# A graph layer on one core: products in four runs a block, float32 work in three, and fewer edges by gather

## The chip, the cores and the metric

The kernel runs on one core of a Trainium2 chip. The metric is the device time of one execution in microseconds; times are compared as medians of several runs on the same chip. TensorE appears in the profile as PE (its matmuls) and PEld (its loads of the stationary operand), VectorE as DVE, ScalarE as ACT, GpSimd as POOL, and the queue that issues most transfers as SP.

## The reference

A graph with 6250 nodes of 64 features and 206250 edges, sorted by their target node `dst`. Each edge carries the normalised features of its source node and 64 features of its own; both are summed into the target node, and a small network follows.

```python
h = jnp.maximum(_layernorm(x, axis=-1), 0.0)
msg = h[src] + edge_attr_64
agg = jax.ops.segment_sum(msg, dst, num_segments=6250)
out = x + jax.nn.relu(agg @ W1 + b1) @ W2 + b2
```

All values are float32; `W1` is 64 x 128, `W2` 128 x 64.

## The kernel before, in words

The sum over edges is split by node. For the first 5502 nodes the source features are not fetched at all. Instead the kernel counts, for three target nodes at a time (a *tile*, a window of up to 128 edges), how many edges come from each of the 6250 nodes, and multiplies these counts by the feature table. For the last nodes the 25 last groups of 1024 edges are gathered from the table by GpSimd (8 gathers a group, each added onto the edge's own features) and summed by matmuls.

The main loop runs over 308 steps of 6 tiles, 14 steps to a *block* of 252 nodes, 22 blocks. A step is written n, its place in the block s (0 to 13). All engines take their instructions in an order that this loop writes out by hand (`tc.manual_schedule`), so the order of the calls in the code is the order in each engine's queue. In a step:

- `count(n)` (L805): six fp8 matmuls of one-hot rows give the counts in `pc`, which has two buffers of PSUM; ACT copies them into `ring` (L811, "eviction" below). The one-hot rows are made by DVE, 18 tiles at a time, every third step (`rows_of_tiles`, L791; every sixth step `encode` comes ahead of it, L772 and L778).
- `products(b - 1, ...)` (L823): 49 matmuls a block in float32r multiply the counts of the block before by the table `h2` into `pv`. `PART` says which of them go into which of the steps 1 to 8. At step 9 DVE adds `pv` to the sums (`add_products`, L852). The ring is long enough that steps 0 to 8 of the next block write to free places.
- The edges' own features: `chunk_hot` (L392, DVE) and `chunk_sum` (L405, 48 float32 matmuls for two chunks of 42 nodes) at s = 6 and 7, 9 and 10, 12 and 13 gather a block's sums in `bank`. `take_sums` (L412, ACT) copies them out at the next block's step 0, and `chunk_place` (L428) adds them to `pv` at its step 2.
- `turn` (L647, L648 on PE; L654, L658 on ACT) brings the codes of 128 tiles into `kq` and `kv`; it stands at steps with s in `TURNS` = (0, 7): in blocks 1 to 21 eight at 0 and five at 7. The codes are unpacked by DVE in the four steps before (`unpack`).
- The small network (`mlp`): `mlp_hidden` (L893, ACT L895), `mlp_product` (L901), `mlp_add` (L906, DVE) and `mlp_store` (L910, SP), one block of nodes at a time, begun at s = 2 or 9 with the later parts 2, 3 and 4 steps on. `residual(g)` loads x for four blocks into one of two slots and `add_b2` adds the bias; the sum goes into one of two buffers `ys`.
- `features_h` (DVE L447, PE L451, ACT L454; the sums are added later at L439) sums two gathered groups, at s = 5 or 11 once the plan says that they have landed. It then queues the gathers of the next two groups on GpSimd (`fetch_h`, L266); the edges' features for them are loaded on SP (`load_h`, L916). The planned clock counts `STEP_US` a step and `GATHER_US` a gather.

After the loop come the products of the last block, cut into fours with the placing and the rest between, then the last group, `add_products`, and the network for the last two blocks of nodes.

Of the kernel before, what the change touches and what calls it, by code (L numbers as in the profile page):

```python
# [22 lines left out]
P = 128  # L23
# [29 lines left out]
GP = 25  # L53
GA = G - GP
EA = GA * P * J

# [17 lines left out]
TURNS = (0, 7)  # L74
TILES = NW * BT
# [29 lines left out]
STEP_US = 1.4  # L105
# [8 lines left out]
def gnn_kernel(ctx: ExitStack, tc: tile.TileContext, x, src_t, dst_t, dst_g, edge, w1, b1, w2, b2, out):  # L114
    nc = tc.nc

    start = [b * BN - (NX * V if b > SB else 0) for b in range(NW)] + [NS]
# [4 lines left out]
    assert max(pairs) == NP and 2 * sum(pairs) == N and start[NW] == NS  # L122
# [245 lines left out]
    for b in range(NW):  # L368
        c0, c1 = start[b] // CN, start[b + 1] // CN
        units += [(b, c, min(c1 - c, GB), i) for i, c in enumerate(range(c0, c1, GB))]  # L370
# [43 lines left out]
    def at_columns(b, a, z):  # L414

        if b % 2 == 0:
            return [(a, z, a)]
        cut = FRESH * SC
        runs = [(a, min(z, cut), a + BN - cut), (max(a, cut), z, max(a, cut) - cut)]
        return [run for run in runs if run[0] < run[1]]  # L420

    def chunk_place(u):
        b, c, n, i = units[u]
        for k in range(n):
            o = (c + k) * CN - start[b]
            at = (i * GB + k) * D
            for a, z, to in at_columns(b, o, o + CN):
                nc.tensor.matmul(pvs[b][k * D:(k + 1) * D, to:to + z - a], by_node[b][:, at:at + D],  # L428
                                 select[:, a - o:z - o], start=False, stop=False)

# [11 lines left out]
    def sum_groups(g, tiles):  # L442
        m = len(tiles)
        pa = bank[:, 512 - GB * W:].rearrange("p (b w) -> p b w", b=GB)
        for b in range(m):
            hot = spare["hotp"][b]
            nc.vector.tensor_tensor(hot, rel_p[:, g - GA + b, :].unsqueeze(2).to_broadcast([P, J, W]),  # L447
                                    iota[:, :W].unsqueeze(1).to_broadcast([P, J, W]), op=OP.is_equal)
            for j in range(J):
                k = j % 2 * D  # L450
                nc.tensor.matmul(pa[k:k + D, b, :], tiles[b][:, j, :], hot[:, j, :],  # L451
                                 start=(j < 2), stop=(j >= J - 2))
# [123 lines left out]
    nc.sync.dma_start(dst_p, dst_t.rearrange("p (g j) -> p g j", j=J)[:, GA:, :])  # L576

# [219 lines left out]
    def count(n):  # L797
# [9 lines left out]
        b, s = divmod(n, STEPS)  # L807
        c = (s if b % 2 == 0 else (STEPS if s < FRESH else 0) + s) * SC
# [8 lines left out]
    def products(b, a, z):  # L817

        if a == 0:
            pvs[b] = ps.tile([P, 512], F32, tag="pv", name="pv")[:, :BN]  # L820
        c = b % 2 * FRESH * SC
        for h in range(a, z):
            nc.tensor.matmul(pvs[b], h2[:, h, :], ring[:, h, c:c + BN], start=(h == 0), stop=(h == HI - 1))  # L823
# [16 lines left out]
    ys = [cut(2 * D)[:NP].rearrange("p (k d) -> p k d", k=2) for _ in range(2)]  # L840
    tail = cut(NX * V)
    spare["sum_p"] = cut(GB * W).rearrange("p (b w) -> p b w", b=GB)
    spare["by_node"] = cut(3 * GB * D)
    hids.append(spare["by_node"][:, :BN])
    spare["hotp"] = [cut(J * W).rearrange("p (j w) -> p j w", j=J) for _ in range(GB)]

    def add_products(b):
        pv = pvs.pop(b)
        n = start[b + 1] - start[b]
# [36 lines left out]
    turn_of = [0]  # L886

    def mlp_hidden(b, k=0):
        n = start[b + 1] - start[b]
        made[b >= NW] = start[b + 1]  # L890
        turn_of[0] ^= 1
# [359 lines left out]
```

## Time and profile before

| what | us |
|---|---|
| median of three runs | 495.16 (491.98 to 500.49) |
| profiled execution, its own time | 493.56 |
| its span, first to last instruction | 491.9 |
| PE busy | 413.5 (84%) |
| DVE busy | 351.4 (71%) |
| ACT busy | 349.7 (71%) |
| POOL busy | 386.9 (79%) |
| first count of the loop starts | 43.05 |
| last two counts of the loop start | 472.43 |

A line of the profile names engine, line of the code, operation, tiles written and read and their shapes; "x48" is the number of instructions merged into one row. In brackets stands how long the engine was idle ahead of it, and who ended that. In the timeline the first number is the start and the second the length; in the table of groups the numbers are busy time, mean length of one in ns, and idle time ahead with its releasers; in the table of waits they are total, times and the longest.

### The profile page before, as it was taken

How to read it: one execution, taken by the hardware profiler on the slowest of the kernel's cores; microseconds unless marked ns; L12 is line 12 of the kernel's file. 1: busy time of each engine (PE TensorE's matmuls, PEld its weight loads, DVE VectorE, ACT ScalarE, POOL GpSimd, SP SyncE). 2: the span in 40 equal slices, each digit the busy share in tenths (PEclk: the TensorE clock that was granted, in tenths of full speed). 3: DMA queues.
4: the chain of work that ended last, by engine and by line, in shares of the span. 5: the costliest groups of instructions: out<-in, count | busy, mean ns of one | idle time of the engine just before them, and what ended most of it. 6: DMA issues, size and time to landing. Idle time of an engine off the chain costs nothing.

```text
span 491.9 us, 17202 instructions
## 1 busy us (share of the span) xinstructions
PE 413.5 (84%) x7172; PEld 371.8 (76%) x7173; DVE 351.4 (71%) x772; ACT 349.7 (71%) x514; POOL 386.9 (79%) x272
## 2 busy tenths in 40 slices
PE   3014779988979997999999998999999989998984
PEld 3013668877878886987888897898888878887974
DVE  4799948985778756688577876698576776687531
ACT  3437977786756868777778798788687766786740
POOL 6756838888888588888888888888888888888880
PEclk9999889999899998999999999999999989999998
DMA  8929455676475848567577768568669567487610
GB/s 225 271 87 325 96 127 124 159 212 153 104 192 117 218 106 210 109 162 198 120 203 174 191 150 217 130 157 230 138 145 248 118 139 191 112 204 169 149 19 18
DMA packets 114099, 78.90 MB, mean 160 GB/s; under 512 B 33864, under 2 KB 109120, under 8 KB 113792
## 3 DMA queue, kind: packets, MB, share of 16 engines
q1 hardware_dynamic: 83624, 65.87, 44.6%
q0 software_dynamic: 30096, 10.36, 18.0%
q10 hardware_dynamic: 295, 1.52, 0.9%
q8 instruction: 58, 0.95, 0.8%
q14 instruction: 26, 0.20, 0.1%
HBM read 73.72 MB, written 3.99 MB: 158 GB/s over the span
## 4 chain that ended last, share of the span: by engine, by line
PE 60%; ACT 16%; DVE 14%; issue 5%; DMA 2%; POOL 1%; DVEq 0%; ACTq 0%
PE pv L823 24%; PE pc L805 19%; ACT ring L811 8%; PE bank L405 8%; DVE hot L791 3%; PE bank L451 3%; ACT kq L654 3%; PE ph L893 2%; PE pv L428 2%; DVE hotf L392 2%; ACT kv L658 2%; DMA sums<-in_dst_g,row_i 1%; DVE sums L852 1%; POOL sums L266 1%; PE po L901 1%
## 5 line engine op out<-in xcount | busy, mean ns | idle before, releaser
L266 POOL DMA_INDIRECT pfeat<-table,src_p x200 | 340.0, 1700 | 64.2 <-issue 53.9
L811 ACT ACTIVATE ring<-pc 128x882 fp32r<-128x882 f32 x308 | 275.1, 923 | 76.8 <-PE pc L805 73.5
L805 PE MATMUL pc<-hot 128*128 128x147 fp8e4 x1848 | 173.6, 234 | 25.4 <-ACT ring L811 13.7
L791 DVE TENSOR_TENSOR hot<-at,of 128x576 int32<-128x576 bf16 (+1 forms) x206 | 161.7, 826 | 29.9 <-PE pc L805 25.3
L823 PE MATMUL pv<-ring,h 128*128 128x252 f32 x1078 | 170.5, 295 | 1.5 <-ACT ring L811 1.5
L805 PEld LDWEIGHTS <-hot 128*128 128x128 fp8e4 x1848 | 127.6, 101 | 46.3 <-issue 20.7
L823 PEld LDWEIGHTS pv<-ring,h 128*128 128x128 f32 x1078 | 139.7, 192 | 1.8 <-ACT ring L811 1.7
L405 PE MATMUL bank<-feat,hotf 128*18 128x64 f32 x3144 | 59.5, 226 | 7.3 <-DVE hotf L392 5.6
L405 PEld LDWEIGHTS bank<-feat,hotf 128*18 128x18 f32 x3144 | 47.7, 101 | 16.4 <-DVE hotf L392 7.0
L852 DVE TENSOR_TENSOR sums<-sums,pv 128x252 f32<-128x252 f32 (+3 forms) x33 | 9.9, 327 | 58.2 <-PE pv L823 56.9
L392 DVE TENSOR_TENSOR hotf<-rel,iota 128x432 f32<-128x432 bf16 x66 | 39.5, 598 | 0.0
L654 ACT ACTIVATE kq<-pk 128x512 bf16<-128x512 f32 (+17 forms) x48 | 18.2, 442 | 17.3 <-PE pk L647 17.3
L772 DVE TENSOR_TENSOR at<-iota_a,kq 128x576 bf16<-128x576 bf16 (+1 forms) x52 | 23.3, 448 | 2.0 <-ACT kq L654 1.7
L778 DVE TENSOR_TENSOR of<-of,kv 128x432 bf16<-128x432 bf16 (+1 forms) x52 | 19.8, 381 | 3.0 <-ACT kv L658 0.2
L266 POOL DMA_INDIRECT words<-packed,first_i x15 | 18.2, 1213 | 4.6 <-issue 3.7
L893 PE MATMUL ph<-sums,w1s 128*128 128x252 f32 (+2 forms) x50 | 17.2, 430 | 5.0 <-ACT over L730 1.8
L266 POOL DMA_INDIRECT sums<-in_dst_g,row_i x15 | 15.4, 1030 | 6.7 <-issue 4.3
L772 DVE TENSOR_TENSOR of<-iota_w,kq 128x432 bf16<-128x432 bf16 (+1 forms) x52 | 19.3, 371 | 0.0
L906 DVE TENSOR_TENSOR after<-po,after 126x128 f32<-126x128 f32 (+2 forms) x25 | 7.2, 287 | 14.5 <-PE po L901 14.0
L454 ACT ACTIVATE after<-bank 128x84 f32<-128x84 f32 (+1 forms) x13 | 3.1, 239 | 19.9 <-PE bank L451 19.9
L895 ACT ACTIVATE after<-ph,b1s 128x252 f32<-128x252 f32 (+2 forms) x25 | 11.9, 475 | 5.3 <-PE ph L893 5.3
L451 PE MATMUL bank<-after,pfeat 128*64 128x42 f32 x400 | 14.5, 232 | 1.2 <-DVE after L447 1.2
(182 smaller groups left out, 315.0 us busy)
## 6 DMA issues: line engine op xcount, KB each, us to landing
feat<-in_edge SPq DMA_DIRECT2D x131, 384.0 KB
pfeat<-in_edge SPq DMA_DIRECT2D x25, 256.0 KB
pfeat<-table,src_p POOLq DMA_INDIRECT x200
out_y<-after SPq DMA_DIRECT2D x23, 63.0 KB
dstn<-in_dst_g SPq DMA_DIRECT2D x1, 1024.0 KB
table<-xl SPq DMA_DIRECT2D x2, 512.0 KB
after<-in_x SPq DMA_DIRECT2D x4, 252.0 KB
packed<-dstn ACTq DMA_DIRECT2D x1, 768.0 KB
```

The lines of the kernel that those rows point to most:

```text
L266: nc.gpsimd.indirect_dma_start(out=rows, out_offset=None, in_=source, in_offset=bass.IndirectOffsetOnAxis(ap=index, axis=0), compute_op=op)
L392: nc.vector.tensor_tensor(hot_of[u][:, :n].rearrange("p c j w -> p (c j) w"), rel[:, c:c + n].rearrange("p c q k -> p (c q k)").unsqueeze( ...
L405: nc.tensor.matmul(bank[q * QP:q * QP + WQ, at:at + D], hot[:, c, j, :], feat[c][:, j, :], start=(k == 0), stop=(k == JP - 1))
L451: nc.tensor.matmul(pa[k:k + D, b, :], tiles[b][:, j, :], hot[:, j, :], start=(j < 2), stop=(j >= J - 2))
L654: nc.scalar.activation(kq[:, q, at:at + n].rearrange("s i k o -> s (i k) o"), pk[:, q, a:a + n].rearrange("s i k -> s (i k)").unsqueeze(2) ...
L772: nc.vector.tensor_tensor(to[:, :n].rearrange("s i k (m o) -> s (i k) m o", o=2), iota_k.rearrange("s (m o) -> s m o", o=2).unsqueeze(1).t ...
L778: nc.vector.tensor_tensor(pairs_of, pairs_of, kv[:, c:c + n].rearrange("s i k o -> s (i k) o").unsqueeze(2) .to_broadcast([P, 2 * n, WE // ...
L791: nc.vector.tensor_tensor(hot[:, :n, c:c + m * A8].rearrange("s i (w a) -> s i w a", a=A8), at[:, o:o + n, k].unsqueeze(2).to_broadcast([P ...
L805: nc.tensor.matmul(pc[:, k, q * K:(q + 1) * K], hot[:, i, :P], hot[:, i, P:P + K], start=True, stop=True)
L811: nc.scalar.activation(to.rearrange("p h (k m) -> p h k m", k=2), pc[:, :, :ST // 2 * K].rearrange("p k (m h) -> p h k m", h=HI), AF.Copy)
L823: nc.tensor.matmul(pvs[b], h2[:, h, :], ring[:, h, c:c + BN], start=(h == 0), stop=(h == HI - 1))
L893: nc.tensor.matmul(ph[:, :n], w1s, agg[:, start[b]:start[b + 1]], start=True, stop=True)
```

## The change

- `PART` puts the 49 products of a block into steps 2, 4, 6 and 8 (12, 12, 12, 13), in place of steps 1 to 8.
- `chunk_place` moves from step 2 to step 7, `mlp_hidden` from 9 to 10 (with the product 3, the add 4 and the store 5 steps on; begun at 2 the parts follow after 2, 3 and 4 steps), `features_h` from 5 and 11 to 7, 10 and 13, and the turns from 0 and 7 to 1 and 7. So the float32 matmuls that are not products stand at steps 7, 10 and 13, but for a network begun at step 2.
- 24 groups are gathered in place of 25, and the last one has four tiles of gathered rows in place of eight: 188 gathers. Four small loads bring its indices into that form.
- The counted part grows by 14 tiles (42 nodes). The last block takes them: its counts run over 17 steps, its products have 294 columns, it has a fourth unit of chunks at step 14. The loop has 311 steps. The 42 nodes form a small block of their own for the network, so that three blocks of nodes remain for the end.
- The network adds onto x where it lies and stores from there; `ys` is gone. `STEP_US` is 1.34.

```diff
-GP = 25
+GP = 24
+JL = 4
-TURNS = (0, 7)
-TILES = NW * BT
+TURNS = (1, 7)
+LAST = 14
+MORE = V * LAST
+TILES = NW * BT + LAST
-STEP_US = 1.4
+STEP_US = 1.34
...
-    start = [b * BN - (NX * V if b > SB else 0) for b in range(NW)] + [NS]
+    start = [b * BN - (NX * V if b > SB else 0) for b in range(NW + 1)] + [NS]
...
+    def nodes(b):
+        return start[b + 1] - start[b] + (MORE if b == NW - 1 else 0)
+    def columns_of_block(b):
+        return BN + (MORE if b == NW - 1 else 0)
+    def block_of(n):
+        b = min(n // STEPS, NW - 1)
+        return b, n - b * STEPS
...
+    def ring_runs(b, a, z):
         if b % 2 == 0:
             return [(a, z, a)]
+        own = FRESH * SC
+        runs = [(0, own, BN), (own, BN, own), (BN, BN + MORE, own - MORE)]
+        return [(max(a, u), min(z, v), c + max(a, u) - u) for u, v, c in runs if max(a, u) < min(z, v)]
...
+    def tiles_of(g):
+        return J if g < G - 1 else JL
...
-            for j in range(J):
+            for j in range(n):
                 k = j % 2 * D
                 nc.tensor.matmul(pa[k:k + D, b, :], tiles[b][:, j, :], hot[:, j, :],
-                                 start=(j < 2), stop=(j >= J - 2))
+                                 start=(j < 2), stop=(j >= n - 2))
...
+    for e in range(J // JL):
+        part, of = slice(e * P * JL // J, (e + 1) * P * JL // J), slice((G - 1) * J + e * JL, (G - 1) * J + (e + 1) * JL)
+        nc.sync.dma_start(src_p[part, (GP - 1) * J:(GP - 1) * J + JL], src_t[:P * JL // J, of])
+        nc.sync.dma_start(dst_p[part, GP - 1, :JL], dst_t[:P * JL // J, of])
...
     def mlp_add(b):
-        po, y = outs[b]
-        nc.vector.tensor_tensor(y[:pairs[b]], po[:pairs[b]], xs_of[b][:pairs[b]], op=OP.add)
+        y = xs_of[b][:pairs[b]]
+        nc.vector.tensor_tensor(y, outs.pop(b)[:pairs[b]], y, op=OP.add)
     def mlp_store(b):
-        y = outs.pop(b)[1]
-        nc.sync.dma_start(out[start[b]:start[b + 1], :].rearrange("(p k) d -> p k d", k=2), y[:pairs[b]])
+        nc.sync.dma_start(out[start[b]:start[b + 1], :].rearrange("(p k) d -> p k d", k=2), xs_of[b][:pairs[b]])
...
-        (NW - 1) * STEPS + 2: [limits],
-        (NW - 1) * STEPS + 3: [limits_found],
+        (NW - 1) * STEPS + 6: [limits],
+        (NW - 1) * STEPS + 7: [limits_found],
...
     def mlp(m, n):
-        for k, f in ((0, mlp_hidden), (2, mlp_product), (3, mlp_add), (4, mlp_store)):
+        wait = 2 if n % STEPS == 2 else 3
+        for k, f in ((0, mlp_hidden), (wait, mlp_product), (wait + 1, mlp_add), (wait + 2, mlp_store)):
             at_step(n + k, f, m)
...
-        for u, s in zip(of_block[b], (7, 10, 13) if b < NW - 1 else (5, 8, 11)):
+        for u, s in zip(of_block[b], (7, 10, 13) if b < NW - 1 else (5, 8, 11, 14)):
...
             for u in of_block[b]:
-                at_step(n + STEPS + 2, chunk_place, u)
+                at_step(n + STEPS + 7, chunk_place, u)
...
-    PART = [0, 0, 6, 10, 16, 23, 30, 36, 43, HI]
+    PART = [0, 0, 0, 12, 12, 24, 24, 36, 36, HI]
...
-        if b and 1 <= s < FRESH:
+        if b and s < FRESH and PART[s] < PART[s + 1]:
             products(b - 1, PART[s], PART[s + 1])
...
-        if s in (2, 9) and ready:
+        if s in (2, 10) and ready:
             mlp(ready.pop(0), n)
...
-            if s in (5, 11) and h_next < G and fetched.get(min(h_next + 1, G - 1), 1e9) + LAND_US <= clock(n):
+            if s in (7, 10, 13) and h_next < G and fetched.get(min(h_next + 1, G - 1), 1e9) + LAND_US <= clock(n):
                 features_h(h_next)
```

More of the change, by code (lines that the diff above doesn't have):

```diff
@@ L52 @@
 ACOLS = N + W + WR
-GP = 25
+GP = 24
 GA = G - GP
 EA = GA * P * J
+JL = 4
+assert (E - (G - 1) * P * J) <= P * JL and J % JL == 0
 HI = 49
@@ L1113, in gnn_kernel @@
     take_sums(b)
-    ends = [m for m in range(NW, NB) if m not in queued and
+    ends = [m for m in range(NW + 1, NB) if m not in queued and
             (start[m + 1] + 30) * (E / N) <= h_next * P * J] + ready
```

75 lines of the change are left out of this document (39 added, 36 removed).

## The prediction

> **What bounds the kernel now.** I read the page first, then the wait table, then the busy time over the second half of the loop, then single steps in the timeline.
>
> ```profile
> span 491.9 us, 17202 instructions
> PE 413.5 (84%) x7172; PEld 371.8 (76%) x7173; DVE 351.4 (71%) x772; ACT 349.7 (71%) x514; POOL 386.9 (79%) x272
> ...
> L266 POOL DMA_INDIRECT pfeat<-table,src_p x200 | 340.0, 1700 | 64.2 <-issue 53.9
> L811 ACT ACTIVATE ring<-pc 128x882 fp32r<-128x882 f32 x308 | 275.1, 923 | 76.8 <-PE pc L805 73.5
> ```
> ```profile
> 230.80:472.80 242.00, 229.38 (x4163) 207.15 (x4160) 175.71 (x373) 185.82 (x265) 204.68 (x123) 0.99 0.68 166
> ```
> ```profile
> PE pc L805 <- ACT ring L811: 13.7, 25, 2.1
> ```
>
> The windows row (PE, PEld, DVE, ACT, POOL busy, clock) covers the last 13 blocks: PE busy 229 of 242 us. PE sets the pace, and it rarely waits for ACT: 13.7 us over the whole span, in 25 places. That small number is what the change puts at risk, so I looked at how close it is. These are PE's rows of blocks 12 to 14 (12 holds neither a turn nor an L451) (a block is 14 steps; each step begins with a count, L805 x6):
>
> ```profile
> 286.13 0.94 PE L805 MATMUL pc<-hot 128*128 128x147 fp8e4 x12
> ...
> 297.40 0.56 PE L805 MATMUL pc<-hot 128*128 128x147 fp8e4 x6
> ...
> 301.36 0.94 PE L805 MATMUL pc<-hot 128*128 128x147 fp8e4 x12 [0.41 <-DVE hot L791]
> ...
> 303.03 0.56 PE L805 MATMUL pc<-hot 128*128 128x147 fp8e4 x6
> ```
> ```profile
> 307.59 0.55 PE L805 MATMUL pc<-hot 128*128 128x147 fp8e4 x6 [0.83 <-ACT ring L811]
> ...
> 311.34 1.13 PE L451 MATMUL bank<-after,pfeat 128*64 128x42 f32 x32
> ...
> 316.84 0.56 PE L805 MATMUL pc<-hot 128*128 128x147 fp8e4 x6
> 317.51 0.69 PE L893 MATMUL ph<-sums,w1s 128*128 128x252 f32 x2
> 318.04 0.55 PE L805 MATMUL pc<-hot 128*128 128x147 fp8e4 x6
> 318.52 0.86 PE L405 MATMUL bank<-feat,hotf 128*18 128x64 f32 x48
> 319.32 0.56 PE L805 MATMUL pc<-hot 128*128 128x147 fp8e4 x6
> 319.71 0.62 PE L901 MATMUL po<-w2s,after 128*126 128x64 f32 x4
> 320.17 0.55 PE L805 MATMUL pc<-hot 128*128 128x147 fp8e4 x6
> 320.88 0.55 PE L805 MATMUL pc<-hot 128*128 128x147 fp8e4 x6 [0.16 <-ACT ring L811]
> ...
> 322.15 0.94 PE L805 MATMUL pc<-hot 128*128 128x147 fp8e4 x12
> ...
> 324.71 0.67 PE L428 MATMUL pv<-select,after 128*64 128x42 f32 x14
> 325.31 0.56 PE L805 MATMUL pc<-hot 128*128 128x147 fp8e4 x6
> 325.67 0.95 PE L823 MATMUL pv<-ring,h 128*128 128x252 f32 x6
> 326.46 0.56 PE L805 MATMUL pc<-hot 128*128 128x147 fp8e4 x6
> ...
> 334.09 0.56 PE L805 MATMUL pc<-hot 128*128 128x147 fp8e4 x6
> ```
> ```profile
> 319.91 2.55 ACT L811 ACTIVATE ring<-pc 128x882 fp32r<-128x882 f32 x3 [0.37 <-PE pc L805]
> 322.75 0.92 ACT L811 ACTIVATE ring<-pc 128x882 fp32r<-128x882 f32 x1 [0.28 <-PE pc L805]
> ...
> 323.93 1.73 ACT L811 ACTIVATE ring<-pc 128x882 fp32r<-128x882 f32 x2
> ```
>
> Prices on PE, from start to start: a count alone 0.39 (319.32 to 319.71), ahead of products 0.36 (325.31 to 325.67), ahead of L405 0.48. Products x6 0.79; one product is 0.12 (0.124 in the long run of the tail, below: 32 from 477.66 to 481.62; I take 0.118), so that starting a run costs 0.05 to 0.08. L405 x48 0.80, L893 0.53, L901 0.46 (319.71 to 320.17), L428 0.60 with 14 matmuls, 0.54 taken as the mean of blocks with 14 and 12.
>
> **The rule that decides.** The counts write pc, two buffers. At step 11 the count starts at 319.32, ACT empties it from 319.91 (0.59 later) for 0.92, and the count two steps on starts at 320.88: 1.56 after the first. Three counts in a row thus take 1.56 us for their first two steps, where PE's own work is 0.78. What hides this today is that nearly every step carries other PE work. Evictions that queue start 0.81 apart (three in 2.55).
>
> **The change, part by part.**
>
> *Products in four runs.* Steps 1 to 8 with runs of 4 to 7 become steps 2, 4, 6, 8 with 12, 12, 12, 13. Four starts fewer: 4 x (0.08 - 0.03), 0.03 being what a count saves ahead of products, so -0.2 us a block. A run of 12 is 0.08 + 12 x 0.118 = 1.50. Steps 0 and 1 now both hold a count alone.
>
> *float32 work in three runs.* L428 moves from step 2 to step 7, L893 from 9 to 10 behind L405, L901 from 11 to 13. Joining spares a start of 0.1 or so (0.48 less 0.39) once or twice a block, and L893 no longer waits for DVE's add of the finished products: 316.84 to 317.51 is 0.67, 0.27 over a count. Together about -0.5.
> The Trainium skill speaks against the joining of L428 and L405: by TensorEngine Tiling (Array Packing), Key Properties, a change of tiling mode drains TensorE, and these two use tiles of 64 and of 32 columns. By that rule this join saves nothing, and the sum would be 2 us higher (21 x 0.1); no trace here has the two side by side.
>
> *What it uncovers.* I write a block out, count 0 at 0. Eviction 0 starts at 0.59, the copy of the bank follows, eviction 1 starts at 1.77 (322.75 to 323.93 is 1.18). Count 1 at 0.39; count 2 must wait for eviction 0: 1.56, PE idle 0.78. Then 3 at 3.42, 4 at 3.82, 5 at 5.68, 6 at 6.08, 7 at 7.94; L428 8.41, L405 8.95, count 8 at 9.75, count 9 at 11.73. Before: 286.13 to 297.40, 11.27. So +0.46.
> From count 9 on: count 10 at 0.39, L405 0.87, L893 1.67, count 11 at 2.20, 12 at 2.59, and 13 waits for eviction 11: 3.76; L405, L901, next count 0 at 5.49. Before: 316.84 to 322.15, 5.31: +0.18. In blocks that are multiples of three, DVE sets count 12:
>
> ```profile
> 299.73 1.57 DVE L791 TENSOR_TENSOR hot<-at,of 128x576 int32<-128x576 bf16 x2
> ```
>
> It stands behind the add and the encode, so count 12 starts 3.96 after count 9 (297.40 to 301.36) in both kernels, and L901, which filled that wait at step 11, comes after it: +0.45. The third kind, with an encode and the one-hot rows of L405 behind it in DVE's queue at step 12, I put at +0.43 by the same reckoning (L405 ready at 4.45, not 4.2).
>
> *Turns at 1 and 7.* Of blocks 1 to 21, eight have one at step 0, which goes to 1, and five one at 7.
>
> ```profile
> 302.01 2.52 ACT L811 ACTIVATE ring<-pc 128x882 fp32r<-128x882 f32 x3 [0.51 <-PE pc L805]
> ...
> 306.57 2.57 ACT L811 ACTIVATE ring<-pc 128x882 fp32r<-128x882 f32 x3
> ```
>
> The third eviction of the first row (0.92 long, at its end) starts at 303.61, the next at 306.57: 2.96, of which 0.81 + 0.37 are eviction and copy and the rest, some 1.77, the turn. At step 1 the turn's 0.62 on PE fills the hole, but eviction 2 then starts at 1.77 + 0.81 + 1.77 = 4.35 and count 4 waits for it until 5.32 in place of 3.82. Block: 13.23. Before: 303.03 to 316.84 less one L451 (1.16 with its start), 12.65. So +0.58. At step 7: 12.4 by the same walk against 11.94 (322.15 to 334.09), +0.45, and 0.2 behind it.
>
> *Sum over blocks 1 to 21.* First part: 8 x 0.46 + 8 x 0.58 + 5 x 0.45 = 10.6. Second: 6 x 0.45 + 7 x 0.18 + 7 x 0.43 + 5 x 0.2 = 8.0, less 1.5 in two blocks whose unpacking moves one step later, out of the way of L405. Together 17. In blocks 1 to 8 other waits are longer and may take some of it in: I take half there, 14 in all. Bounds: -15 (all of 0.7 x 21 saved, no wait uncovered) and +19 (nothing taken in, no gain from the unpacking).
>
> *24 groups, four tiles.* 12 gathers fewer, 12 x (1.70 + 0.30) = 24 us of POOL.
>
> ```profile
> 477.66 4.03 PE L823 MATMUL pv<-ring,h 128*128 128x252 f32 x32
> ```
> ```profile
> 479.21 1.48 POOL L266 DMA_INDIRECT pfeat<-table,src_p  x1 [0.30 <-issue]
> ...
> 481.62 0.88 PE L451 MATMUL bank<-after,pfeat 128*64 128x42 f32 x16
> ```
>
> The last gather ends at 480.7 and the L451 that reads it starts right behind PE's products, without a wait. So POOL is just covered: the 24 us buy nothing now, but a loop more than 1 us shorter would have needed them. Only the last L451 leaves the tail: -0.8. In the loop L451 follows L405 at 7, 10 or 13 (-0.1 each), its one-hot rows can be late behind an encode: -2 to +3, taken as 0.
>
> *14 tiles more.* Three steps with little beside the count, at eviction pace (1.56 for two, and L405 for one chunk): +2.4. Products of the last block have 294 columns: 49 x 0.12 x 42/252, +1.0. A third small layer at the end (L893, L901, an add, a store): +0.7.
>
> *Layers over x.* The add writes where x lay, so the next load of x waits on SP for a store; behind it stand the loads of edge features (L383), fetched two units ahead. Only one load comes one step behind its store: 0 to 3 us, taken as 0. The four small index loads at the start go out while SP is idle before 35.48, and DVE reads src_p at 30.01: 0 to 2, taken as 0.
>
> ```profile
> 35.48 0.99 SPq L383 DMA_DIRECT2D feat<-in_edge  x2
> ```
> ```profile
> 30.01 0.26 DVE L580 TENSOR_SCALAR src_hi<-src_p 128x200 int32<-128x200 int32 x1
> ```
>
> Sum: 14 - 0.8 + 2.4 + 1.0 + 0.7 = +17.3. The profiled execution took 493.56 (span 491.9); 493.56 + 17.3 = 511. The median of the runs is 495.16, so this is 3.2% above it.
>
> **The rivals.**
> A, on the other side: the holes fill. If PE's saving of 0.7 a block lasts and no new wait for evictions appears, -14.7 + 3.3 gives 482. For it: PE is the pace-setter, 13.7 us of waits in all. Against: the 1.56 rule, which holds whatever PE does. It decides if count 2 starts less than 1.2 after count 0 in most blocks.
> B: savings and holes cancel, because waits of other kinds (DVE, the first blocks) already cover most of them: +3.3 from the end and some 2 from the loop, 499.
> C: as forecast, and the late one-hot rows and the stores on SP cost their upper bounds: 511 + 3 + 3 + 2, 519.
> D: the clock. Idle holes twice a block lower the granted clock (0.99 in the window above). In the opening, behind long idle times, a count spans 0.90 where it spans 0.56 later:
>
> ```profile
> 47.57 0.90 PE L805 MATMUL pc<-hot 128*128 128x147 fp8e4 x6 [1.48 <-ACT ring L811]
> ```
>
> If five counts in half the blocks lost 0.34 each, +18: 529. Against: behind the wait of 0.83 in block 13 the counts keep 0.56. The Trainium skill describes such a drop from short idle times between groups of matmuls that cycle through PSUM (TensorE: Matmul & The Clock Gate, A second HAM failure mode: psum-queue depth-cycling); by that rule the time would be this one, and the trace so far does not bear it out.
>
> **How the numbers follow.** Forecast 0.52, A 0.16, B 0.24, C 0.05, D 0.03. The measurement can tell about 2% from no change, so the bounds are 485.3 and 505.1. Faster 0.16 (A), same 0.26 (B and a little of the forecast), slower 0.58. The range runs from 484, short of A's 482, to 519, where C stands: it leaves out most of A, and D. The forecast's own range is 505 to 516.
>
> **What would show it.** In the changed kernel's waits, PE pc behind ACT ring should rise from 13.7 us to 25 or more; count 2 should start 1.56 after count 0 in blocks without a turn, and count 4 about 5.3 after it in blocks with one. Products should show in runs of 12 and 13 of 1.5 and 1.6 us. The last gather should end 15 us or more before the last products. It is wrong if steps 0 to 2 and 11 to 13 show no wait, or if the blocks of the second half are shorter than 18 us on average.

## The result and the profile after

The changed kernel takes 522.07 us (519.84 to 525.28) where the kernel before, beside it, takes 494.74 (491.98 to 500.49): the ratio is 1.058, with an interval of 1.049 to 1.067. The forecast was 511: slower is right, the size is not. Ratios below are always against runs of the kernel before on the same chip at the same time; the last four runs met a stretch in which that kernel itself took 514, so for them the ratio alone counts.

The profiled execution took 519.84, its span is 517.9. The page of the changed kernel, then its row over the same 13 blocks (9 to 21) that the row of before covered, with the columns length, PE, PEld, DVE, ACT and POOL busy, clock, DMA share and GB/s:

```profile
span 517.9 us, 17208 instructions
...
PE 412.0 (80%) x7194; PEld 372.1 (72%) x7195; DVE 353.2 (68%) x776; ACT 347.6 (67%) x517; POOL 365.9 (71%) x260
```
```profile
240.25:494.33 254.08, 224.93 (x4125) 204.67 (x4125) 178.19 (x374) 183.05 (x263) 188.19 (x114) 0.99 0.64 156
```

PE has not more to do: 224.9 us in place of 229.4. But it is idle for 29.2 us of these blocks, where it was idle for 12.6. The clock is the same 0.99. The table of waits of the changed kernel says for whom PE waits (total, times, longest):

```profile
PE pc L839 <- ACT ring L845: 32.2, 46, 2.1
...
PE bank L424 <- DVE hotf L411: 14.0, 26, 1.5
...
PE ph L925 <- DVE sums L467: 5.6, 3, 2.2
```

The first row was 13.7 before and is the one that the forecast lived on. The other two were not in it: the wait for `hotf` was 5.6 (6 times), the one for a group's sums 1.0. By the steps in which the rows stand, in blocks 1 to 20, 9.0 us of the first are at step 13 (2.3 before) and 13.3 at steps 2 and 4; of the second, 4.9 us are at step 10 (0.8 before), 4.8 at step 7 (0.8) and 3.8 at step 13 (4.0); of the third, 1.2 are behind the loop, as the 1.0 was before. The first two show in PE's timeline of a block without a turn (start, length; the new line numbers are L839 count, L845 eviction, L857 products, L424 `chunk_sum`, L453 `chunk_place`, L925 and L933 the layer, L480 a gathered group):

```profile
299.88 0.95 PE L839 MATMUL pc<-hot 128*128 128x147 fp8e4 x12
301.44 0.54 PE L839 MATMUL pc<-hot 128*128 128x147 fp8e4 x6 [0.62 <-ACT ring L845]
301.78 1.65 PE L857 MATMUL pv<-ring,h 128*128 128x252 f32 x12
...
308.21 0.67 PE L453 MATMUL pv<-select,after 128*64 128x42 f32 x14
308.81 0.87 PE L424 MATMUL bank<-feat,hotf 128*18 128x64 f32 x48
309.61 0.56 PE L839 MATMUL pc<-hot 128*128 128x147 fp8e4 x6
309.97 1.79 PE L857 MATMUL pv<-ring,h 128*128 128x252 f32 x13
311.60 0.94 PE L839 MATMUL pc<-hot 128*128 128x147 fp8e4 x12
312.85 0.87 PE L424 MATMUL bank<-feat,hotf 128*18 128x64 f32 x48 [0.31 <-DVE hotf L411]
313.65 0.69 PE L925 MATMUL ph<-sums,w1s 128*128 128x252 f32 x2
314.18 0.55 PE L839 MATMUL pc<-hot 128*128 128x147 fp8e4 x6
315.55 0.94 PE L839 MATMUL pc<-hot 128*128 128x147 fp8e4 x12 [0.82 <-DVE hot L825]
```

Count 2 starts 1.56 after count 0 (299.88 to 301.44), with PE idle for 0.62: the forecast's rule to the hundredth. At step 10 the sums of the chunks start at 312.85, 0.86 after their count (311.60 plus 0.39, two counts being one row). Before, it was 0.48 (318.04 to 318.52). The reason stands in DVE's timeline of the changed kernel:

```profile
311.80 0.48 DVE L886 TENSOR_TENSOR sums<-sums,pv 128x162 f32<-128x162 f32 x2 [4.12 <-PE pv L857]
312.20 0.60 DVE L411 TENSOR_TENSOR hotf<-rel,iota 128x432 f32<-128x432 bf16 x1
```

The one-hot rows (L411) are queued behind the add of the products (L886), and the add waits for the products. The kernel before has the same two operations in the same order, but there the layer stood at step 9, between the add and the sums of step 10. In the changed kernel step 9 is a count alone.

Over blocks 9 to 20 I took the mean length of every step from the starts of the counts:

| steps | 0 to 8 | 9 | 10 | 11 | 12 | 13 | 9 to 13 | block |
|---|---|---|---|---|---|---|---|---|
| before | 12.49 | 1.27 | 1.28 | 1.36 | 0.57 | 1.67 | 6.15 | 18.65 |
| changed | 12.87 | 0.44 | 2.39 | 0.64 | 1.01 | 2.38 | 6.86 | 19.72 |
| rows early | 12.87 | 0.44 | 2.07 | 0.60 | 1.00 | 2.32 | 6.42 | 19.29 |
| layers back | 13.02 | 1.21 | 1.36 | 1.04 | 0.63 | 1.99 | 6.23 | 19.24 |

(The two last rows are experiments below.) Two thirds of what a block of the second half lost, it lost in its last five steps.

### The profile page after: what moved, and what is told of

Same layout as the page of the kernel before. It is cut to its first block, busy times and chain, and to the rows that moved or that the text cites. A ratio compares the mean times of both kernels' runs of the same rounds, so it can differ in the third digit from the quotient of the medians.

```text
span 517.9 us, 17208 instructions
## 1 busy us (share of the span) xinstructions
PE 412.0 (80%) x7194; PEld 372.1 (72%) x7195; DVE 353.2 (68%) x776; ACT 347.6 (67%) x517; POOL 365.9 (71%) x260
## 4 chain that ended last, share of the span: by engine, by line
PE 51%; DVE 13%; ACT 12%; issue 3%; DVEq 0%; ACTq 0%
PE pv L857 19%; PE pc L839 13%; PE bank L424 8%; ACT ring L845 7%; DVE hot L825 4%; PE po L933 3%; DVE hotf L411 2%; PE bank L480 2%; ACT kq L688 2%; PE ph L925 2%; PE pv L453 2%; ACT kv L692 1%; DVE sums L886 1%; DVE of L812 1%; DVE at L806 1%
## 5 line engine op out<-in xcount | busy, mean ns | idle before, releaser
L284 POOL DMA_INDIRECT pfeat<-table,src_p x188 | 318.2, 1693 | 76.6 <-issue 53.4
L845 ACT ACTIVATE ring<-pc 128x882 fp32r<-128x882 f32 x310 | 271.5, 922 | 90.1 <-PE pc L839 88.2
L839 PE MATMUL pc<-hot 128*128 128x147 fp8e4 x1862 | 162.7, 233 | 43.3 <-ACT ring L845 32.2
L825 DVE TENSOR_TENSOR hot<-at,of 128x576 int32<-128x576 bf16 x208 | 163.3, 827 | 27.5 <-PE pc L839 23.4
L839 PEld LDWEIGHTS <-hot 128*128 128x128 fp8e4 x1862 | 129.7, 101 | 61.2 <-issue 40.2
L857 PE MATMUL pv<-ring,h 128*128 128x252 f32 (+1 forms) x1078 | 152.0, 291 | 0.9 <-ACT ring L849 0.9
L857 PEld LDWEIGHTS pv<-ring,h 128*128 128x128 f32 x1078 | 135.8, 193 | 1.3 <-ACT ring L849 1.1
L424 PE MATMUL bank<-feat,hotf 128*18 128x64 f32 x3168 | 59.7, 225 | 14.1 <-DVE hotf L411 14.0
L424 PEld LDWEIGHTS bank<-feat,hotf 128*18 128x18 f32 x3168 | 47.8, 101 | 23.2 <-DVE hotf L411 19.3
L886 DVE TENSOR_TENSOR sums<-sums,pv 128x252 f32<-128x252 f32 (+4 forms) x34 | 10.0, 323 | 79.7 <-PE pv L857 77.2
L411 DVE TENSOR_TENSOR hotf<-rel,iota 128x432 f32<-128x432 bf16 (+1 forms) x67 | 39.9, 595 | 0.0
L688 ACT ACTIVATE kq<-pk 128x512 bf16<-128x512 f32 (+18 forms) x48 | 18.5, 454 | 18.6 <-PE pk L681 18.6
L938 DVE TENSOR_TENSOR after<-po,after 126x128 f32<-126x128 f32 (+3 forms) x26 | 7.5, 290 | 23.3 <-PE po L933 22.5
L925 PE MATMUL ph<-sums,w1s 128*128 128x252 f32 (+3 forms) x52 | 16.6, 408 | 8.5 <-DVE sums L467 5.6
L927 ACT ACTIVATE after<-ph,b1s 128x252 f32<-128x252 f32 (+3 forms) x26 | 11.8, 461 | 15.6 <-PE ph L925 15.3
L483 ACT ACTIVATE after<-bank 128x84 f32<-128x84 f32 x12 | 3.0, 246 | 22.1 <-PE bank L480 22.1
```

Source lines behind the costliest of these rows:

```text
L284: nc.gpsimd.indirect_dma_start(out=rows, out_offset=None, in_=source, in_offset=bass.IndirectOffsetOnAxis(ap=index, axis=0), compute_op=op)
L411: nc.vector.tensor_tensor(hot_of[u][:, :n].rearrange("p c j w -> p (c j) w"), rel[:, c:c + n].rearrange("p c q k -> p (c q k)").unsqueeze( ...
L424: nc.tensor.matmul(bank[q * QP:q * QP + WQ, at:at + D], hot[:, c, j, :], feat[c][:, j, :], start=(k == 0), stop=(k == JP - 1))
L688: nc.scalar.activation(kq[:, q, at:at + n].rearrange("s i k o -> s (i k) o"), pk[:, q, a:a + n].rearrange("s i k -> s (i k)").unsqueeze(2) ...
L825: nc.vector.tensor_tensor(hot[:, :n, c:c + m * A8].rearrange("s i (w a) -> s i w a", a=A8), at[:, o:o + n, k].unsqueeze(2).to_broadcast([P ...
L839: nc.tensor.matmul(pc[:, k, q * K:(q + 1) * K], hot[:, i, :P], hot[:, i, P:P + K], start=True, stop=True)
```

## Experiments: the three parts alone

**Products in four runs, nothing else.** On the kernel before:

```diff
-    PART = [0, 0, 6, 10, 16, 23, 30, 36, 43, HI]
+    PART = [0, 0, 0, 12, 12, 24, 24, 36, 36, HI]
```


> The kernel before with one part of the change: the products in runs of 12, 12, 12, 13 at steps 2, 4, 6, 8. Theory (two buffers of counts: three counts with nothing between them take 1.56 us for two steps): count 2 starts 1.56 after count 0 in blocks without a turn, 0.78 lost and 0.3 saved there; in blocks with a turn at step 0 its own work fills the hole and about 0.3 is saved. 13 x 0.5 - 8 x 0.3 = +4 us on before. Rival 1 (long runs are what costs, by the clock or by holding up VectorE's add): +10 or more, in all blocks alike. Rival 2 (only starts of runs count): -4.

502.19 us, ratio 1.019 (1.014 to 1.024), +8.3. In blocks 9 to 20 steps 0 to 8 take 12.86 in place of 12.49, as in the full change. The +8.3 is twice the theory's +4 and neither rival's number, but only part of it is in the loop: from the first count of block 1 to that of block 21 the trace takes 394.9 in place of 389.7, 5.2 more. Another 2.7 lie behind the last count, where this profile has a lower granted clock; these are the windows of the kernel before and of this one (length first, the clock is the third number from the end):

```profile
472.80:491.90 19.10, 11.21 (x100) 9.55 (x97) 2.18 (x8) 3.24 (x7) 6.67 (x5) 0.88 0.10 17
```
```profile
478.40:500.20 21.80, 13.92 (x101) 12.10 (x98) 2.18 (x8) 3.25 (x7) 3.74 (x3) 0.73 0.07 14
```

Why the clock differs there is not shown. In this kernel PE also waits 2.9 us for the chunk rows of step 7; before it was 0.8, and 0.2 in the next kernel.

**The float32 moves, nothing else.** On the kernel before, the placing at 7, layers at 2 and 10, groups at 7, 10 and 13:

```diff
-            at_step(n + STEPS + 2, chunk_place, u)
+            at_step(n + STEPS + 7, chunk_place, u)
-        if s in (2, 9) and ready:
+        if s in (2, 10) and ready:
-            if s in (5, 11) and h_next ...
+            if s in (7, 10, 13) and h_next ...
```


> The kernel before with only the float32 matmuls moved: the placing to step 7, the layer to steps 2 and 10 (product 3 steps on from 10), the gathered groups to 7, 10, 13; products as before. Theory (VectorE's queue: at step 9 it waits for the last products, and the one-hot rows of the unit at step 10 stand behind that add; the layer at step 10 stands behind a late add of gathered sums): TensorE waits 0.36 ahead of the unit at step 10 in most blocks, 2.2 us two or three times ahead of the layer, and 0.6 at step 13: +10 to +13 us on before. Rival (the cost of the change lies in the products alone): -5 to 0.

516.03 us, ratio 1.044 (1.038 to 1.050), +22: about twice the theory's price. This is the part that was mis-sized. PE waits 10.1 us for evictions at step 13 (2.3 before), 4.1 us for the rows of step 10 (0.8 before) and 5.3 us for sums (1.0 before).

**Groups, tiles and layers over x, with products, turns, placing, layers and groups at the steps of before.**

> The changed kernel with the products, turns, layers, placing, groups' steps and the planned step time of before: what is left is 24 groups with four tiles in the last, 14 tiles more in the last block, and layers over x. Theory: three steps, wider products and a third layer at the end: +3 us on before (+2 to +5), the last gather ending 15 us or more before the last products. Rival (stores that hold up the loads of x, or the four small loads): +8 or more.

499.55 us, ratio 1.012 (1.005 to 1.019), +5.6: a little above the theory's range and below the rival's. In its trace none of it is in blocks 1 to 20 (388.1 us, before 389.7). From the first count of block 21 to the end it takes 46.0 (before 37.3, in the changed kernel 41.0), and part of that is the clock in the tail of its profile, where four products take 1.3 us and in the changed kernel 0.8; the two profiles, this kernel first:

```profile
479.98 1.35 PE L857 MATMUL pv<-ring,h 128*128 128x294 f32 x4
```
```profile
501.41 0.81 PE L857 MATMUL pv<-ring,h 128*128 128x294 f32 x4
```

The three parts alone add up to 36 us, the change to 27. As the profiles of the first and the third have a tail at a low clock that the changed kernel's has not, it stays open how much of these 9 us is overlap.

## Experiments: the waits on DVE

**The rows one step earlier.** On the changed kernel, the one-hot rows for step 10 are made ahead of the add:

```diff
-            at_step(n + s - 1, chunk_hot, u)
+            at_step(n + s - (2 if s == 10 else 1), chunk_hot, u)
```


> The changed kernel, only that the one-hot rows of the group summed at step 10 are made one step earlier, ahead of DVE's add of the products. Theory (the rows stand behind that add in DVE's queue, so the group's matmuls start 0.79 to 0.86 us after the start of the count instead of 0.47): about 0.36 us less in each of some 20 blocks, 7 us less, 515. Rival (the 0.36 is covered: step 11 or 12 then waits for its count's buffer instead): 0 to 1 us less, 521 to 522.

510.36 us, ratio 1.034 (1.030 to 1.039): 11.7 less, more than the theory. PE's timeline and waits in this kernel:

```profile
305.83 0.94 PE L839 MATMUL pc<-hot 128*128 128x147 fp8e4 x12
306.70 0.87 PE L424 MATMUL bank<-feat,hotf 128*18 128x64 f32 x48
```
```profile
PE pc L839 <- ACT ring L845: 29.9, 43, 2.1
...
PE bank L424 <- DVE hotf L411: 9.1, 9, 1.8
...
PE ph L925 <- DVE sums L467: 5.2, 3, 2.0
```

The sums now start 0.48 after their count in all of blocks 1 to 20; the mean was 0.79 in the changed kernel and 0.53 before. By the traces these blocks get 9.9 shorter together. Blocks 1, 6 and 15 give 1.9, 1.8 and 1.5 of it: in the changed kernel's trace they hold steps at a low clock, and here fewer or none. The other 17 get 0.28 shorter each, about what the rows were late by (0.31). So a good half of the gain is the order on DVE. Whether the rest follows from it, by shorter waits, or is a difference of the clock between two executions, is not shown.

**The sums of a group one step later**, so that the layer at step 10 is not behind them:

```diff
-                add_later(n + 3)
+                add_later(n + (4 if s == 7 else 3))
```


> The changed kernel, only that the sums of a group made at step 7 are added one step later, at step 11. Theory (the layer's first product at step 10 waits 2.2 us each time for that add, which stands in DVE's queue behind encodings and one-hot rows): the three waits of 5.6 us in all go, 5 us less, 517. Rival (the layer then waits for whatever else is in that queue, or the next consumer of DVE does): 0 to 2 us less, 520 to 522.

517.48 us, ratio 1.047 (1.040 to 1.054), 4.6 less: the theory's number. What it took away looks like this in the changed kernel, PE and DVE:

```profile
188.21 0.87 PE L424 MATMUL bank<-feat,hotf 128*18 128x64 f32 x48 [0.31 <-DVE hotf L411]
191.25 0.62 PE L925 MATMUL ph<-sums,w1s 128*128 128x210 f32 x2 [2.18 <-DVE sums L467]
...
193.26 0.90 PE L839 MATMUL pc<-hot 128*128 128x147 fp8e4 x6 [0.62 <-ACT ring L845]
```
```profile
189.27 1.58 DVE L825 TENSOR_TENSOR hot<-at,of 128x576 int32<-128x576 bf16 x2
190.76 0.43 DVE L467 TENSOR_TENSOR sums<-sums,after 128x42 f32 x2
```

A group of 32 small matmuls at step 7 has its sums ready in time, but the 0.43 us add stands in DVE's queue behind 1.58 of one-hot rows, and PE stands behind it.

**Both.**

> The changed kernel with both orders on DVE mended: the rows of step 10 one step earlier, and the sums of a group of step 7 one step later. Theory (both waits are the whole of what the forecast lacked, and they add up): 11.7 and 4.6 less, 505 to 508, a ratio of 1.022 to 1.028. Rival (with the rows early the sums are no longer late, so the two are one): 509 to 511, a ratio of 1.030 to 1.035.

Ratio 1.043 (1.034 to 1.052). The theory's range (to 1.028) lies outside, and the rival's is only touched. Both waits did go down (for the rows from 14.0 to 10.7 us, for the sums from 5.6 to 1.2, which is the wait behind the loop), but in this stretch PE also waited for what the profile can only call issue, in rows that the changed kernel's table of waits does not have:

```profile
PE pc L839 <- issue: 4.9, 9, 1.1
...
PE bank L424 <- issue: 3.4, 10, 0.5
```

So this run decides between neither, and how far the two overlap stays open.

**Layers where they were** (on the changed kernel, 2 and 9 with the second product two steps on):

> The changed kernel, only that the layers stand where they stood before: first product at step 2 or 9, second two steps later. Theory (at 10 and 13 the layer leaves steps 9, 11 and 12 with counts alone, so that count 13 waits for eviction 11, and at 10 it stands behind the rows and sums that DVE still has to make): about 0.7 us less in some 12 blocks and 4 to 5 us of waits for sums, 10 to 13 us less, 509 to 512. Rival (the waits move to the next consumer of DVE): 519 to 522.

508.69 us, ratio 1.026 (1.020 to 1.033), 13.4 less: the theory. By the medians this gives back most of all single pieces; its interval overlaps that of the rows made early. PE's waits there:

```profile
PE pc L839 <- ACT ring L845: 23.8, 41, 2.1
...
PE bank L424 <- DVE hotf L411: 11.9, 15, 2.1
```

With the layer at step 9 the rows are ready in time though nothing on DVE was moved (0.55 as mean start; 1.2 us of waits are left at step 10), and no layer in the loop waits for sums any more. The largest piece is another: in blocks 1 to 20 the waits for evictions at step 13 fall from 9.0 to 2.6 us, because steps 9 and 11 no longer hold counts alone. That wait, for eviction 11, the forecast had. The last row of the table above shows steps 9 to 13 back at 6.23.

**Groups at 5 and 11 as before** (on the changed kernel):

> The changed kernel, only that gathered groups are multiplied at steps 5 and 11 as before. Theory (a group multiplied at step 7 has its sums added at step 10, ahead of which the layer's first product waits; at 5 and 11 it does not): the 5.6 us of waits go and nothing else moves: 516 to 517. Rival (as step 5 holds a count alone in the changed kernel, the 1.2 us of a group also fill it, and L424 at 10 starts sooner): 508 to 512. Second rival (rows of a group late behind an encode): 522 to 525.

513.11 us, ratio 1.036 (1.030 to 1.042), 9 less: between theory and first rival. The sums no longer come between (in the loop no wait for L467), and waits for rows fall to 10.5, but mostly it is steps 9 to 13 again, 6.32.

**Float32 moves alone, rows early.**

> The kernel before with the float32 moves alone, and the rows of step 10 made one step earlier. Theory (what the float32 moves cost beyond 10 to 13 us is the group at step 10 waiting for rows behind DVE's add and encode): 8 to 12 us less than the moves without it, 504 to 508. Rival (the excess is the empty steps 9, 11 and 12 of PE, whatever DVE does): 514 to 517.

Ratio 1.040 (1.030 to 1.051) against 1.044 without: the theory's range (1.020 to 1.028) lies outside. The start of the sums did move, to 0.47 everywhere, but here waits called issue stand in the way too: 8.6 us ahead of L405, where the run without has none. So this does not settle it either; what it does show is that the early rows leave the waits for evictions at step 13 (11.5 us in blocks 1 to 20).

**Float32 moves without the layers':**

> The kernel before with the float32 moves but without the layers': placing at 7, gathered groups at 7, 10 and 13, the layers where they were. Theory (the layer that leaves steps 9 and 11 is most of the 22 us: it covered DVE's rows and the ring's waits there): a ratio of 1.010 to 1.020, some 5 to 10 us over before. Rival (the placing or the groups cost it): 1.035 or more.

Ratio 1.014 (1.007 to 1.021): the theory. If the ratios of the two stretches may be compared, the layers' move is two thirds of what the float32 moves cost (1.044); the 13.4 us above, from an undisturbed stretch, agree.

**Placing at step 2 as before** (on the changed kernel):

> The changed kernel, only that the chunks of the block before are placed at step 2 as before. Theory (placing is 0.6 us of PE work in either place, and neither place holds a wait that it could fill): 521 to 523. Rival (in blocks whose rows are not ready at step 7 its 0.6 us covered a wait there): 524 to 530. Second rival (joined to the sums at 7 it costs a drain of PE): 518 to 520.

Ratio 1.056 (1.044 to 1.067), the changed kernel's own. Where it stands is worth nothing that these runs can tell.

## Experiments: the waits on ACT

**Evictions in halves.** On the changed kernel, the two banks of a count are separate buffers, four in all:

```diff
-        pc = ps.tile([P, 2, 512], F32, tag="pc", name="pc")
+        pc = [ps.tile([P, 512], F32, tag="pc", name="pc", bufs=4) for _ in ...]
...
-            nc.scalar.activation(to.rearrange(...), pc[:, :, ...], AF.Copy)
+            for k in range(2):
+                nc.scalar.activation(to[:, :, k * SC // 2:(k + 1) * SC // 2], pc[k][...], AF.Copy)
```


> The changed kernel, only that a count's two banks are separate buffers, each evicted by an operation of its own, so that the count two steps on can start on the first bank when the first half is evicted. Theory (three counts with nothing between them lose 0.78 us, because a buffer comes free only 1.51 us after its count began): the first half comes free about 0.5 us earlier, the waits of matmuls for ring evictions fall from 32 us to under 18, 10 to 20 us less, 502 to 512. Rival (ACT gets 308 more operations, and its fixed part of some 0.1 to 0.2 us each makes the evictions themselves later): 522 or more, up to 545.

520.63 us, ratio 1.054 (1.047 to 1.060): 1.4 less, nothing clear of noise, above the theory's range and just short of the rival's. Waits and groups of this kernel:

```profile
PE pc L840 <- ACT ring L847: 12.9, 22, 1.9
```
```profile
L847 ACT ACTIVATE ring<-pc 128x441 fp32r<-128x441 f32 x620 | 302.3, 597 | 61.1 <-PE pc L840 58.8
```

The waits for evictions did fall, from 32.2 to 12.9, and the time did not. Two halves take 1.19 us of ACT for 0.92 (less where they queue and overlap: 302.3 us in all, and 271.5 in the changed kernel), and what the next count gains, the products or a later count give back: over blocks 9 to 20 steps 1, 3 and 12 get 0.31, 0.19 and 0.30 shorter, steps 2 and 13 get 0.19 and 0.35 longer. From the first count of block 1 to that of block 21 PE is idle 9.9 us less (44.3 in place of 54.2) but busy 7.4 us more (365.8 in place of 358.3), so that this stretch gains only 2.4; and in the tail of this profile the clock is lower (0.71, in the changed kernel's 0.90). A sum of waits in a table is not a sum of time.

**Turns at 0 and 7.**

> The changed kernel, only that turns stand at steps 0 and 7. Theory (with a turn at 1 count 4 waits for eviction 2 until 5.3 us after count 0; with one at 0 count 3 waits until about 4.6, and the layer at step 2 no longer waits for the turn's copy of po): 0.4 us less in eight blocks and 1.7 us of the layer's waits, 4 to 5 us less, 517 to 518. Rival (the turn's copies delay the evictions as much wherever they stand): 521 to 523.

524.01 us, ratio 1.060 (1.055 to 1.066): the rival, a little above its range. ACT's copies of a turn hold up the evictions as much at step 0; the wait only changes its step.

**Products one step earlier**, runs at 1, 3, 5 and 8 (on the changed kernel):

```diff
-    PART = [0, 0, 0, 12, 12, 24, 24, 36, 36, HI]
+    PART = [0, 0, 12, 12, 24, 24, 36, 36, 36, HI]
```


> The changed kernel with its first three runs of products one step earlier, at steps 1, 3, 5 and 8; run lengths and all else unchanged. Theory (the hole at steps 0 to 2): count 2 no longer waits, 0.78 less in the 13 blocks without a turn at step 1, some 0.4 less in the other 8: 12 to 14 us less than the changed kernel. Rival (the length of the runs costs, by the clock or by what VectorE waits for): no change within 2 us.

511.67 us, ratio 1.036 (1.032 to 1.041), 10.4 less: nearly the theory. A run at step 1 fills the hole ahead of count 2.

## Experiments: a version that beats both

The groups, tiles and layers over x of the change and its `STEP_US`, everything else as before, and the products in four runs at steps 1, 3, 5 and 7:

```diff
+    PART = [0, 0, 12, 12, 24, 24, 36, 36, HI, HI]
```


> The 24 groups, the four tiles, the 14 tiles more and the layers over x of the change, with the steps of placing, layers, features and turns of before, and the products in four runs at steps 1, 3, 5 and 7, none at 8. Theory (the counts without work between them are what four runs lose by; alternating steps leave no three such counts in a row, and the products end earlier): the price of groups and tiles, 5.6 us, less 0.2 us a block for fewer starts and 0.3 us for every hole filled: 485 to 496, at or below the kernel before. Rival (four long runs themselves cost the 8.3 us of the products-only kernel, wherever they stand): 505 to 509.

481.90 us (479.78 to 482.92), ratio 0.976 (0.970 to 0.981): faster than before by 13, and than the changed kernel by 40. That is 3 us below the theory's range. From the first count of block 1 to that of block 21 it takes 372.4 (before 389.7), and 9.0 of the 17.3 are gained in blocks 1 to 8; why so much there is not shown. Its row for blocks 9 to 21, and its waits:

```profile
221.65:455.79 234.14, 223.45 (x4134) 203.40 (x4128) 176.65 (x371) 182.03 (x264) 198.48 (x118) 1.00 0.69 171
```
```profile
PE pc L839 <- ACT ring L845: 18.2, 37, 2.1
...
PE bank L424 <- DVE hotf L411: 2.7, 5, 1.0
```

PE is busy for 223.5 us of 234.1, idle for 10.7. It has the same work as in the changed kernel within 1.5 us; all the rest is waiting.

**The same products on the kernel before**, with its 25 groups:

> The kernel before, only that the products stand in four runs, at steps 1, 3, 5 and 7. Theory (PE's loop gets some 13 us shorter, but the last gathers of 25 groups end when they did, at about 480 us of the span, and the last groups must follow them): 487 to 493, a gain of at most 1.5%; DVE or PE shows a wait for the gathers at the end that the kernel before does not have. Rival (the gathers are not what sets the end): 478 to 482, as much less as the loop. Second rival (four long runs cost in themselves): 500 or more.

491.97 us, ratio 0.994 (0.990 to 0.998): the theory. The reason is what PE waited for ahead of L451 (total, times, longest), here and then in the kernel before, and the start of the last gather here:

```profile
PE bank L451 <- DMA pfeat<-table,src_p: 7.6, 7, 1.7
```
```profile
PE bank L451 <- DVE after L447: 1.2, 2, 0.9
```
```profile
479.62 1.48 POOL L266 DMA_INDIRECT pfeat<-table,src_p  x1 [0.30 <-issue]
```

The shorter loop runs into the gathers and waits for them seven times. From the first count of block 1 to that of block 21 it takes 382.3 (before 389.7), but the last gather ends at 481.10, where it ended at 480.69 before, and PE waits for what it fetched until 482.56. The tail has a low clock here too (0.73), but even so the last group waits for the gather. With 24 groups that is gone: in the faster kernel the last gather and the group that reads it stand as follows (POOL and PE), almost 7 us apart.

```profile
459.48 1.55 POOL L284 DMA_INDIRECT pfeat<-table,src_p  x1 [0.30 <-issue]
```
```profile
467.86 0.90 PE L480 MATMUL bank<-after,pfeat 128*64 128x42 f32 x24
```

Neither half of this version gains much by itself (ratios of 0.994 and 1.012); together they gain 2.4%.

## Why the prediction was right, and where it was wrong

**Right: what PE waits for, and its sizes up to step 9.** Count 2 stands 1.56 after count 0. As a sign this alone says little, for in block 12 of the kernel before it was 1.57 (286.13 to 287.70), filled there by six products:

```profile
286.88 0.94 PE L823 MATMUL pv<-ring,h 128*128 128x252 f32 x6
```

What tells is that PE is now idle for 0.62 of it. In the block shown above count 9 should start 11.73 after count 0 and starts 11.72 after it (299.88 to 311.60). In a block with a turn, count 4 should start 5.32 after count 0; it starts at 323.08 after 317.79, 5.29, here:

```profile
317.79 0.87 PE L839 MATMUL pc<-hot 128*128 128x147 fp8e4 x11
...
323.08 0.55 PE L839 MATMUL pc<-hot 128*128 128x147 fp8e4 x6 [1.41 <-ACT ring L845]
```

Runs of 12 products take 1.65 by the rows, 1.48 to the next start, as said (1.50). Steps 0 to 8 were priced at +10.6 for 21 blocks, 0.50 each; in blocks 9 to 20 they came to 0.38.

**Right: the end and the gathers.** From the first count of block 21 to the end it was 37.3 and is 41.0: +3.6, forecast +3.3. That it fits so well is in part luck: the forecast has no term for the clock in the tail, and with a low one the same stretch took 46.0 (the groups alone). The last gather ends at 479.24, the last products at 508.16, 29 us later (15 or more was asked):

```profile
477.49 1.75 POOL L284 DMA_INDIRECT pfeat<-table,src_p  x1 [0.31 <-issue]
```
```profile
507.22 0.94 PE L857 MATMUL pv<-ring,h 128*128 128x294 f32 x5
```

That the 24 us of POOL buy nothing now, and would be needed by a shorter loop, both came true: 7.6 us of waits with 25 groups in a shorter loop.

**Joining: it costs nothing, and at step 7 it spares nothing.** At step 7 L453, L424 and the next count start 0.60 and 0.80 apart (308.21, 308.81, 309.61), which is what the walk of the block took for the two apart. The 0.1 that the part on the float32 work had put for a start spared is not seen there. The Trainium skill's rule (TensorEngine Tiling (Array Packing), Key Properties: a change of tiling mode drains TensorE) is not contradicted, as L428 was followed by a change of mode before too. With the placing undone the ratio is the same.

**Wrong: the sum over blocks 1 to 21, taken as 14.** From the first count of block 1 to that of block 21 it was 389.7 and is 412.5, +22.9. By the forecast's own shares (0.8 a block, half of that in blocks 1 to 8) blocks 1 to 8 were to cost 3 and blocks 9 to 20 10; they cost 9.9 and 12.9. Three steps of it failed:

1. "L893 no longer waits for DVE's add of the finished products", and, in the walk from count 9 on, "L405 0.87": the wait for DVE's rows was put at nothing. The wait did leave the layer, and the next in line got it: the rows of step 10 are queued behind the same add, and without the layer in step 9 nothing covers them. In steps 9 to 13 the walk gave +0.38 a block, or +0.31 with the unpacking; blocks 9 to 20 lost 0.71. The walk took L405 as ready at 0.87; the row says 1.25 (311.60 to 312.85). Rows early take 0.44 a block off these steps in blocks 9 to 20 (some of it is the clock of block 15) and leave 0.27 over before, which is near the walk's own 0.31; over the whole kernel they give 11.7 us back, the clock's share included. The layer at step 9 gives back 13.4, but that takes away the wait for eviction 11 as well, which the walk had. By the span, the kernel with the rows early is 16.2 us over before (508.1 less 491.9), where the forecast had 17.3.
2. A group at step 7 adds its sums at step 10, ahead of the layer. I had asked for the one-hot rows of L451 only, and took 0. It is 4.4 us of waits in the loop, and 4.6 us of time.
3. Blocks 1 to 8, where I took half off, as "other waits may take some of it in": they lost 9.9 us together (165.9 to 175.8), and 6.1 of it in two blocks. Block 6 holds the wait of 2.18 for sums and a low clock behind it. Block 1 has a lower clock than before, 0.74 for 0.92, and with the rows early it takes 22.1 at 0.91; its windows, before and changed:

```profile
64.87:86.20 21.33, 19.01 (x370) 17.29 (x369) 14.14 (x38) 15.79 (x21) 12.22 (x8) 0.92 0.47 113
```
```profile
64.42:88.42 24.00, 21.13 (x370) 19.46 (x369) 14.00 (x38) 15.55 (x21) 13.53 (x8) 0.74 0.42 105
```

The other six lost 0.6 each, of the 0.8 that was halved to 0.4. So what the sum lacked here is the clock more than the half; why block 1 got the lower clock stays open.

That the kernel with the rows early comes so close to the forecast is in part luck: it still has 4.0 us of waits for sums in the loop that the forecast lacked, so other terms were a little too high.

**The rivals.** A (holes fill) and B (savings and holes cancel) fell; A's 482 is what the version with runs at odd steps reached, but that is another kernel, with the float32 work where it was. C's 519 is nearest to the measured time, by luck: its late one-hot rows were other rows than those it named. D (a lower clock behind short holes) is not it: 0.99 over the second half. The changed kernel does have steps at a low clock, after long waits and not after short holes: behind the wait of 2.18 in block 6 a count takes 0.90 (193.26) where it takes 0.55. The rule of the Trainium skill that stood behind D (TensorE: Matmul & The Clock Gate, A second HAM failure mode: psum-queue depth-cycling) would have had it behind the 0.62 holes twice a block, and there the counts keep 0.54 to 0.56.

**What stays open.** How far the two waits on DVE overlap, since their common run met other waits; how much of what the early rows give back is the clock; and why PE gets busier when evictions go by halves, beyond the 31 us that ACT paid for it.

## What to carry to other kernels

When a step is moved, list what it stood in front of on every engine, not only what it waited for: the layer at step 9 covered an add on DVE and the one-hot rows queued behind it, and its matmuls kept counts from standing alone; moving it cost 13 us. Spread the work of the engine that sets the pace so that no two buffers' worth of steps goes without it; the same four runs cost 8 us at steps 2, 4, 6, 8 (5 in the loop) and cost nothing at 1, 3, 5, 7. And two edits that each do nothing may be halves of one gain: a shorter loop gained 0.6% until the gathers were shortened as well, then 2.4%.

## What the runs showed of the hardware beyond that

- A count's eviction in two operations of 441 elements takes 2 x 597 ns, in one of 882 it takes 923: some 270 ns for a second operation that stands alone; over all counts, with queued ones overlapping, it is 31 us, 0.1 each.
- The clock in the tail differs between profiles: four products of 294 columns at 0.81 us (the changed and the fastest kernel) or at 1.35 (the groups alone), with the same wait of 0.9 us ahead of the first four in both. So a difference of 3 us between two kernels can lie in the tail alone.
- In the last four runs PE waited inside and ahead of groups of 48 small matmuls for something that the profile shows no releaser for. This is the row of `chunk_sum` in the changed kernel with the placing undone (total, times, longest); the changed kernel itself has no such row:

```profile
PE bank L424 <- issue: 7.9, 27, 0.5
```
